# Graph layer in one pass over sorted edges: eight slot segments, clears in half-megabyte pieces, last layers in stages

## The chip, the cores and the metric

The kernel runs on one core of one Trainium2 chip. The metric is the time of one launch in microseconds (us), the median of several runs. A profiled execution, with its own time, stands beside them.

## The reference

There are 12500 nodes with 128 features, and 412500 edges (`src`, `dst`, 20 attributes, a weight), sorted by `dst`. All arithmetic is float32.

```python
h = jnp.maximum(_layernorm(x, axis=-1), 0.0)
# the graph layer, with idx_i = src (summed into) and idx_j = dst (gathered from)
hw  = h @ W_in2f
Wij = ssp(f_ij @ W_f1 + b_f1) @ W_f2 + b_f2        # ssp(x) = softplus(x) - log 2
x_ij = hw[idx_j] * (Wij * rcut_ij[:, None])
agg = jax.ops.segment_sum(x_ij, idx_i, num_segments=N)
out = ssp(agg @ W_o1 + b_o1) @ W_o2 + b_o2
return x + out
```

The gather runs over sorted nodes, so that neighbouring edges read neighbouring rows. The sum runs over `src`, which is in no order.

## The kernel before

**Edges to slots.** The edges are worked in order of `dst`, in 806 chunks of 512 (a *step* each); four chunks make a group, and there are 202 groups. For a chunk the kernel computes the edge messages (128 edges by 128 features, four times) and writes each message, with the place of its node within its block in a 129th column, to a row of its own in a table in HBM. A block is 128 nodes; there are 98 blocks, and four of them are a *quad* (25 quads). The row is found by counting: `rank` keeps in PSUM (`free`) how many rows of each block are taken. The write is an indirect DMA from GpSimd, four a step (L745; a *put* below), 3224 in all.

**Segments.** The groups are cut into segments (`SEGS`), each with its own slot table. In a table every block has `T` tiles of 128 rows (one more in the blocks where the segment's own `dst` range lies). With 64, 56, 32, 24, 14 and 12 groups, T is 12, 11, 7, 5, 3 and 3, and the tables have 1208, 1118, 710, 506, 310 and 304 tiles.

**Clears.** Rows that may stay unwritten must read as zeros. `clear` lists DMAs that write a zero tile over the middle part of every block's rows; a piece is at most 128 half blocks by ZN x ZR = 32 rows of 516 bytes, some 2.1 MB. The dict `zeros` holds at which step each is issued on SyncE's queue (L961): the first segment's before step 108, the second's from step 128 to 246, all others from 128 to 470. The first put into a segment waits for its clears (the first segment's for step 128).

**Collecting.** When a segment is full, `Collect` adds its table up: `load` (L783) brings a unit of up to 6 tiles into SBUF, `compare` (L794, VectorE) makes a 0/1 matrix from the 129th column, and `add` (L807, TensorE) multiplies: each tile adds into the accumulator `acc` of its quad. `acc` has one buffer. At a quad's end `keep` (L824, VectorE) adds it to the sums `agg`. The units of all segments but the last are spread over the steps by a planner, which works out a rate in tiles a step for each: 5.39 for the first segment (steps 265 to 488), and from then on 8.16 and 8.24. The last segment is collected after the last step.

**A step.** `step(k)` issues, in this order, on each engine in its own queue: the loads for later chunks and units; `blocks` for chunk k+7; `hidden_end` (L631); `window` (L706); `message` for chunk k (L739 and L741, which multiplies into one of four `o` tiles of two chunks each, then the four puts); `value` (L726, L730) and `picked` (L714, L719) for chunk k+1; `compare` of the units; `rank` for chunk k+6; `hidden`; `add` of the unit before; `rank_end`. At a segment's last chunk `rank_end` also reduces the counts for a flag (L693 to L701), and at a segment's first groups `columns` (L578 to L606) prepares new columns. This order is written out by hand (`tc.manual_schedule()`). `aside` runs `make_h` (layer norm and the first product) for later nodes beside the first 200 steps.

**After the last step.** The last segment's units are loaded, compared and added, and each finished quad goes through `finish`: load x on ScalarE's queue (L387), the product with W_o1 (L389), softplus (L366 to L373), the product with W_o2 (L398), two adds on VectorE (L401, L402) and the store (L403). This part stands outside the manual schedule: a scheduler places its instructions.

If the flag shows that a count went over a bound, a second way of computing everything (`anyway`) is run behind `tc.If`; it shares `finish`.

Of the kernel before, what the change touches and what calls it, by code (L numbers as in the profile page):

```python
# [9 lines left out]
F32 = mybir.dt.float32  # L10
# [4 lines left out]
ALU = mybir.AluOpType  # L15
PSUM = bass.MemoryType.PSUM

P = 128
TG = 16
CH = 512  # L20
NCHUNK = TG * P // CH
QT = CH // P
SEGS = (64, 56, 32, 24, 14, 12)
RW = P + 1
VIEWS = 16
BG = 8
ZR = 8
ZN = 4
WR = 32
UT = 6  # L30
BIG = float(1 << 11)
# [4 lines left out]
def ceil_div(a, b):  # L36
    return -(-a // b)
# [3 lines left out]
def gnn_kernel(  # L41
# [20 lines left out]
    nc = tc.nc  # L62
    N, D = x.shape
    NG, _, RBF, _ = f_t.shape
# [62 lines left out]
    NQ = ceil_div(N, QN)  # L127
# [15 lines left out]
    state = ctx.enter_context(tc.tile_pool(name="state", bufs=1))  # L143
# [13 lines left out]
    for c0 in range(0, NC, P):  # L157
        n = min(P, NC - c0)
# [14 lines left out]
    for q in range(NQ):  # L173
        cs = slice(quad_of.index(q), quad_of.index(q) + quad_of.count(q))
# [19 lines left out]
    wo2 = load(w_o2, [P, P], "wo2")  # L194
# [3 lines left out]
    bo2 = load(b_o2[None, :].to_broadcast([P, P]), [P, P], "bo2")  # L198
# [5 lines left out]
    def spread(t, n):  # L204
        return t[:, None, :].to_broadcast([t.shape[0], n, P])
# [14 lines left out]
    flag = const.tile([1, 1], I32, name="flag")  # L220
# [35 lines left out]
    bad = const.tile([1, NFLAG], F32, name="bad")  # L256
    nc.vector.memset(bad, 0.0)
    sums = tc.dram_tile([SUMT * P, P], F32, name="sums")
    segs = [Segment(k) for k in range(len(SEGS))]

# [107 lines left out]

    def softplus_end(a, r):

        nc.scalar.activation(a, a, AF.Exp, scale=-1.0)
        nc.scalar.activation(a, a, AF.Ln, bias=half, scale=0.5)
        nc.vector.tensor_add(r, r, a)  # L373

    def finish(t0, n, sT, edge, quad, psum):

        n0 = t0 * P
        full = min(n, N // P - t0)
        rest = N - n0 - full * P if full < n else 0
        xo = quad.tile([P, QT, P], F32, name="xo")  # L380
        pieces = []
        if full:
            pieces.append((P, slice(0, full), slice(n0, n0 + full * P)))
        if rest:
            pieces.append((rest, slice(full, n), slice(n0 + full * P, N)))
        for p, cs, rows in pieces:
            nc.scalar.dma_start(xo[:p, cs, :], x[rows, :].rearrange("(c p) f -> p c f", p=p))  # L387
        z = psum.tile([P, 2, CH], F32, name="z_out", tag="z")[:, 0, :n * P]
        nc.tensor.matmul(z, wo1, sT, start=True, stop=True)  # L389
        a = edge.tile([P, QT, P], F32, name="a_out")  # L390
        r = edge.tile([P, QT, P], F32, name="r_out")
        a_n = a[:, :n, :].rearrange("p c f -> p (c f)")
        r_n = r[:, :n, :].rearrange("p c f -> p (c f)")
        softplus_parts(a_n, r_n, z, bo1)
        softplus_end(a_n, r_n)
        v = psum.tile([P, QT, P], F32, name="v_out", tag="v", bufs=3)
        for i in range(n):
            nc.tensor.matmul(v[:, i, :], r[:, i, :], wo2, start=True, stop=True)  # L398
        for p, cs, rows in pieces:
            xi = xo[:p, cs, :]  # L400
            nc.vector.tensor_add(xi, xi, spread(bo2[:p, :], xi.shape[1]))  # L401
            nc.vector.tensor_add(xi, xi, v[:p, cs, :])  # L402
            nc.sync.dma_start(out[rows, :].rearrange("(c p) f -> p c f", p=p), xi)  # L403


    def anyway(edge, quad, psum):
        none = edge.tile([P, SUMT // parts * P], F32, name="none", bufs=1)
        nc.vector.memset(none, 0.0)
        rows = sums[:, :].rearrange("(p a c) f -> a p (c f)", p=P, a=parts)
# [3 lines left out]
        with tc.For_i(0, NG, 1) as g:  # L413
            f = edge.tile([P, CH], F32, name="f")
# [23 lines left out]
            for t in range(TG):  # L438
                c, i = divmod(t, QT)
# [19 lines left out]
                v = psum.tile([P, P], F32, name="v", bufs=3)  # L459
# [4 lines left out]
                m = quad.tile([P, P], F32, name="m")  # L464
# [9 lines left out]
        for t0 in range(0, NTILE, QT):  # L474
            n = min(QT, NTILE - t0)
            o = quad.tile([P, QT, P], F32, name="s_out")
            nc.sync.dma_start(o[:, :n, :], sums[t0 * P:(t0 + n) * P, :].rearrange("(c p) f -> p c f", p=P))
            tps = psum.tile([P, QT, P], F32, name="t_out", tag="nodes")
            for i in range(n):
                nc.tensor.transpose(tps[:, i, :], o[:, i, :], ident)  # L480
            sT = quad.tile([P, QT, P], F32, name="sT")
            nc.scalar.activation(sT[:, :n, :], tps[:, :n, :], AF.Copy)
            finish(t0, n, sT[:, :n, :].rearrange("p c f -> p (c f)"), edge, quad, psum)


    with tc.tile_pool(name="edge", bufs=2) as edge, tc.tile_pool(
        name="quad", bufs=3
# [3 lines left out]
        kept = {}  # L491
# [8 lines left out]
        def clear(seg):  # L500

            todo = []

            def put(b, e, low):

                half = seg.tiles(b) * P // 2
                v = seg.views[VIEWS][seg.row(b):seg.row(e), :].rearrange(
                    "(r c) f -> r (c f)", c=half)
                for q in range(0, 2 * (e - b), P):
                    n = min(P, 2 * (e - b) - q)  # L510
                    for r in range(low, half - low, ZN * ZR):
                        w = min(ZN * ZR, half - low - r)
                        todo.append((
                            v[q:q + n, r * RW:(r + w) * RW].rearrange("r (k f) -> r k f", f=ZR * RW),
                            zero[:n, None, :].to_broadcast([n, w // ZR, ZR * RW])))

            full = (NBLK - 1) // BG * BG
            for b, e in ((0, seg.b0), (seg.b0, min(seg.b1, full)), (seg.b1, full)):
                if b < e:
                    put(b, e, seg.low)  # L520

            for b in range(full, NBLK):
                low = seg.low if b < NBLK - 1 else seg.low_last
# [375 lines left out]
        zeros = {}  # L899
        units = {}  # L900
        collects = [Collect(seg) for seg in segs]
        AHEAD = 3

        seg = segs[0]
        todo = clear(seg)
        for i, d in enumerate(todo):
            zeros.setdefault(i * (seg.cleared - 20) // len(todo), []).append((seg, d))
        todo = clear(segs[1])
        for i, d in enumerate(todo):
            zeros.setdefault(seg.cleared + i * (seg.c1 - 10 - seg.cleared) // len(todo),  # L910
                             []).append((segs[1], d))
        todo = [(seg, d) for seg in segs[2:] for d in clear(seg)]
        for i, d in enumerate(todo):
            zeros.setdefault(segs[0].cleared + i * (segs[2].c0 - 10 - segs[0].cleared)
                             // len(todo), []).append(d)

        at = [seg.c1 + 9 for seg in segs[:-1]]
        work = [sum(seg.tiles(b) for b in range(NBLK)) for seg in segs[:-1]]
# [2 lines left out]
        while len(rate) < len(at):  # L921
            n = len(at) - len(rate)
            j = max(range(n), key=lambda j: sum(work[j:n]) / (end - at[j]))
# [25 lines left out]
        with tc.manual_schedule():  # L949
# [17 lines left out]
                step(k, now)  # L967
                next(aside, None)
            summed[0].add(summed[1])
        last = collects[-1]  # L970
        for u in range(len(last.units)):
            last.load(u)
            last.compare(u)
            last.add(u)
            for done in last.kept:
                finish(*done, edge, quad, psum)
            last.kept = []
        worst = state.tile([1, 1], F32, name="worst")
        nc.vector.tensor_reduce(worst, bad, axis=mybir.AxisListType.X, op=ALU.max)
        nc.vector.tensor_copy(flag, worst)  # L980

    missed = nc.values_load(flag[0:1, 0:1], min_val=0, max_val=P)
    with tc.If(missed > 0):
        with tc.tile_pool(name="any_e", bufs=2) as edge, tc.tile_pool(
            name="any_q", bufs=2
# [51 lines left out]
```

## Time and profile before

| what | value |
|---|---|
| time, median of 3 runs | 4383.54 us (4381.74 to 4402.45) |
| profiled execution, time and span | 4396.31 us, 4394.5 us |
| TensorE, VectorE, ScalarE, GpSimd busy | 82%, 71%, 53%, 71% |
| granted TensorE clock, mean | 0.855 |
| DMA | 829 MB, mean 189 GB/s |
| first put, last put (start) | 85.1 us, 4220.6 us |
| put, mean duration | 964 ns, x3224 |
| clears issued (L961) | 164, from 78.9 to 2441.6 us |

The profiled execution is 13 us above the median. PE is TensorE's matmuls, PEld its weight loads, DVE VectorE, ACT ScalarE, POOL GpSimd, SPq SyncE's DMA queue. A row of a group gives line, engine, operation, tiles, count, then busy time and mean duration, then the idle time before it and who ended that; a row of the waits gives who waited for whom, in all, how often, and the longest; a row of a table by stage gives a stretch, its length, each engine's busy time with its number of instructions, then the granted clock, the DMA engines' busy share and GB/s. Start times of single instructions are from the timeline.

### The profile page before, as it was taken

How to read it: one execution, taken by the hardware profiler on the slowest of the kernel's cores; microseconds unless marked ns; L12 is line 12 of the kernel's file. 1: busy time of each engine (PE TensorE's matmuls, PEld its weight loads, DVE VectorE, ACT ScalarE, POOL GpSimd, SP SyncE). 2: the span in 40 equal slices, each digit the busy share in tenths (PEclk: the TensorE clock that was granted, in tenths of full speed). 3: DMA queues.
4: the chain of work that ended last, by engine and by line, in shares of the span. 5: the costliest groups of instructions: out<-in, count | busy, mean ns of one | idle time of the engine just before them, and what ended most of it. 6: DMA issues, size and time to landing. Idle time of an engine off the chain costs nothing.

```text
span 4394.5 us, 72656 instructions
## 1 busy us (share of the span) xinstructions
PE 3607.4 (82%) x22558; PEld 2618.3 (60%) x22558; DVE 3140.1 (71%) x6637; ACT 2332.5 (53%) x4685; POOL 3114.6 (71%) x3288
## 2 busy tenths in 40 slices
PE   3767776777777888888788889999899998989877
PEld 2544444444444666666566567777677776767666
DVE  5766666566555776767667678787888878888766
ACT  3655555555555555555555555555555555545424
POOL 2777777677777777777777777777777777777620
PEclk9776666667666898899998899999999999999999
DMA  5766547888765666765876566666666766766666
GB/s 139 192 178 230 174 128 197 223 223 230 183 208 135 177 178 183 238 193 166 257 197 174 150 179 187 194 195 185 189 188 183 199 191 185 193 188 191 172 180 192
DMA packets 498071, 829.10 MB, mean 189 GB/s; under 512 B 170680, under 2 KB 288300, under 8 KB 497676
## 3 DMA queue, kind: packets, MB, share of 16 engines
q1 hardware_dynamic: 378950, 602.34, 51.2%
q0 software_dynamic: 103168, 213.15, 14.7%
q10 hardware_dynamic: 15558, 8.89, 0.7%
q8 instruction: 182, 2.98, 0.3%
q14 instruction: 213, 1.74, 0.1%
HBM read 425.03 MB, written 398.98 MB: 188 GB/s over the span
## 4 chain that ended last, share of the span: by engine, by line


## 5 line engine op out<-in xcount | busy, mean ns | idle before, releaser
L745 POOL DMA_INDIRECT slots<-o,slot x3224 | 3108.4, 964 | 1106.3 <-issue 803.6
L719 ACT ACTIVATE hg<-picked,rcut 128x128 f32<-128x128 f32 x3224 | 920.8, 369 | 1372.0 <-PE picked L714 1323.5
L807 PEld LDWEIGHTS acc<-to,m 128*128 128x128 f32 x8312 | 1078.7, 205 | 353.8 <-issue 187.7
L807 PE MATMUL acc<-to,m 128*128 128x128 f32 x8312 | 1154.6, 294 | 92.3 <-DVE agg L824 47.3
L730 PEld LDWEIGHTS v<-wf,r 128*128 128x128 f32 x6448 | 918.1, 220 | 303.7 <-issue 303.7
L730 PE MATMUL v<-wf,r 128*128 128x128 f32 x6448 | 1088.2, 320 | 0.0
L616 PE MATMUL z<-f,wf 20*128 20x512 f32 x1612 | 524.2, 726 | 217.5 <-DVE r L631 190.9
L794 DVE TENSOR_TENSOR to<-count_ps,m 128x768 f32<-128x768 f32 (+3 forms) x829 | 657.9, 812 | 51.8 <-PE acc L807 27.7
L619 ACT ACTIVATE a<-z,bf 128x1024 f32<-128x1024 f32 x403 | 449.1, 1114 | 426.7 <-PE z L616 426.7
L660 DVE TENSOR_REDUCE top<-free 128x4 f32<-128x392 f32 x806 | 447.2, 555 | 211.7 <-PE free L655 210.4
L631 DVE SCALAR_TENSOR_TENSOR r<-z,nbf,a 128x1024 f32<-128x1024 f32 x403 | 514.6, 1277 | 94.2 <-ACT a L625 92.5
L741 DVE TENSOR_TENSOR o<-v,hg 128x512 f32<-128x512 f32 x806 | 547.2, 679 | 2.8 <-ACT hg L719 2.1
L739 DVE COPY o<-place 128x8 f32<-128x8 f32 x403 | 80.4, 200 | 650.9 <-DMA slots<-o,slot 650.6
L714 PE MATMUL picked<-near,at 96*128 96x128 bf16 x3224 | 356.4, 240 | 218.0 <-DVE o L741 215.7
L625 ACT ACTIVATE a<-a,half 128x1024 f32<-128x1024 f32 x403 | 468.4, 1162 | 0.0
L636 DVE TENSOR_TENSOR inb<-count_ps,blk 128x392 f16<-128x392 f32 x806 | 445.7, 553 | 0.0
L726 PE MATMUL v<-bf_p,ones_b 3*128 3x512 bf16 x806 | 350.1, 434 | 104.1 <-DVE o L741 93.9
L620 ACT ACTIVATE a<-a 128x1024 f32<-128x1024 f32 x403 | 425.9, 1057 | 12.8
L714 PEld LDWEIGHTS <-at 96*128 96x128 bf16 x3224 | 275.7, 109 | 256.2 <-DVE o L741 224.6
L616 PEld LDWEIGHTS z<-f,wf 20*128 20x128 f32 x1612 | 142.4, 206 | 388.9 <-issue 186.3
L687 PE MATMUL free<-inb,rest_of 128*128 128x392 f16 x806 | 303.1, 376 | 55.0 <-DVE top L660 53.8
L706 DVE TENSOR_TENSOR at<-rel,prow 96x512 bf16<-96x512 bf16 x806 | 331.1, 411 | 0.0
(107 smaller groups left out, 1416.2 us busy)
## 6 DMA issues: line engine op xcount, KB each, us to landing
m<-slots SPq DMA_DIRECT2D x371, 387.0 KB
rel<-rel_d SPq DMA_DIRECT2D x202, 384.0 KB
m<-slots SPq DMA_DIRECT2D x172, 322.5 KB
m<-slots SPq DMA_DIRECT2D x212, 258.0 KB
slots<-o,slot POOLq DMA_INDIRECT x3224
slots<-zero SPq DMA_DIRECT2D x24, 2064.0 KB
f<-in_f_t SPq DMA_DIRECT2D x404, 80.0 KB
slots<-zero SPq DMA_DIRECT2D x22, 1032.0 KB
```

What stands on the lines that cost most here:

```text
L616: nc.tensor.matmul(z[:, k, :], wf1[rows, :], self.f[rows, :], start=True, stop=True)
L619: nc.scalar.activation(a, z, AF.Abs, bias=bf1)
L625: nc.scalar.activation(a, a, AF.Ln, bias=half, scale=0.5)
L631: nc.vector.scalar_tensor_tensor(r, z, nbf1, a, op0=ALU.max, op1=ALU.add)
L660: nc.vector.tensor_reduce(self.top[:, c * QT:(c + 1) * QT], free_v, axis=mybir.AxisListType.X, op=ALU.max)
L714: nc.tensor.matmul(ps[:, i, :], at[:, i * P:(i + 1) * P], near, start=True, stop=True)
L719: nc.scalar.activation(hg[:, i, :], ps[:, i, :], AF.Copy, scale=self.rcut[:, j:j + 1])
L730: nc.tensor.matmul(v[:, i, :], r[:, i * P:(i + 1) * P], wf2, start=False, stop=True, skip_group_check=True)
L741: nc.vector.tensor_mul(o[:, :, :P], v, hg)
L745: put = nc.gpsimd.indirect_dma_start(out=views[j % VIEWS], out_offset=bass.IndirectOffsetOnAxis(ap=self.slot[:, j:j + 1], axis=0), in_=o[: ...
L794: nc.vector.tensor_tensor(to[:, :n, :], count_ps[:, None, :].to_broadcast([P, n, P]), self.m[u][:, :n, P:].to_broadcast([P, n, P]), op=ALU ...
L807: nc.tensor.matmul(self.acc[b // QT][:, i, :], m[:, j, :P], to[:, j, :], start=t == 0, stop=t == self.seg.tiles(b) - 1)
```

## The change

Three things are changed.

- `SEGS` has eight segments instead of six. T becomes 13, 10, 6, 3, 3, 2, 2 and 2, and the tables have 1314, 1012, 612, 310, 310, 212, 204 and 206 tiles. The planner's rates become 6.32 tiles a step for the first segment (from step 281) and 8.235 from step 489 to the end. The segments with T = 3 are collected in steps 686 to 760, those with T = 2 in steps 761 to 811.
- `ZN` goes from 4 to 1, so that a clear is at most 0.53 MB. There are 636 of them with 158.5 MB, instead of 164 with 147.3 MB. A new loop spreads them evenly by number, in runs, so that each segment's are out before it needs them.
- `finish` becomes a generator with five `yield`s. After the last step, now inside the manual schedule, the stages of several quads are interleaved: while a quad's sums are added, the quad in front has its W_o1 product and activations, the one before that its softplus add, the one before that its W_o2 product, and the one before that the last add and the store. The x loads go to SyncE's queue two quads ahead, and b_o2 is added to x on GpSimd one quad ahead. The last segment's `compare` is one unit and its `load` three units ahead. The flag is reduced before this part.

```diff
-SEGS = (64, 56, 32, 24, 14, 12)
+SEGS = (68, 52, 30, 14, 14, 8, 8, 8)
-ZN = 4
+ZN = 1
...
-    def finish(t0, n, sT, edge, quad, psum):
+    def finish(t0, n, sT, quad, psum):
...
-        xo = quad.tile([P, QT, P], F32, name="xo")
+        xo = quad.tile([P, QT, P], F32, name="xo", bufs=6)
...
-            nc.scalar.dma_start(xo[:p, cs, :], x[rows, :].rearrange("(c p) f -> p c f", p=p))
+            nc.sync.dma_start(xo[:p, cs, :], x[rows, :].rearrange("(c p) f -> p c f", p=p))
+        yield
+        for p, cs, rows in pieces:
+            xi = xo[:p, cs, :]
+            nc.gpsimd.tensor_add(xi, xi, spread(bo2[:p, :], xi.shape[1]))
+        yield
...
         softplus_parts(a_n, r_n, z, bo1)
-        softplus_end(a_n, r_n)
+        softplus_logs(a_n)
+        yield
+        nc.vector.tensor_add(r_n, r_n, a_n)
+        yield
         v = psum.tile([P, QT, P], F32, name="v_out", tag="v", bufs=3)
         for i in range(n):
-            nc.tensor.matmul(v[:, i, :], r[:, i, :], wo2, start=True, stop=True)
+            nc.tensor.matmul(v[:, i, :], r_n[:, i * P:(i + 1) * P], wo2, start=True, stop=True)
+        yield
         for p, cs, rows in pieces:
             xi = xo[:p, cs, :]
-            nc.vector.tensor_add(xi, xi, spread(bo2[:p, :], xi.shape[1]))
             nc.vector.tensor_add(xi, xi, v[:p, cs, :])
             nc.sync.dma_start(out[rows, :].rearrange("(c p) f -> p c f", p=p), xi)
...
+        clears = [(seg, d) for seg in segs for d in clear(seg)]
+        due = [seg.cleared - 20 if seg is segs[0] else seg.c0 - 10 for seg in segs]
+        todo = [sum(seg is s for s, _ in clears) for seg in segs]
+        t0, i = 0, 0
+        while i < len(segs):
+            j = max(range(i, len(segs)), key=lambda j: sum(todo[i:j + 1]) / (due[j] - t0))
+            n = sum(todo[i:j + 1])
+            for m in range(n):
+                zeros.setdefault(t0 + m * (due[j] - t0) // n, []).append(clears.pop(0))
+            t0, i = due[j], j + 1
...
-        for u in range(len(last.units)):
-            last.load(u)
-            last.compare(u)
-            last.add(u)
-            for done in last.kept:
-                finish(*done, edge, quad, psum)
-            last.kept = []
...
+            for u in range(len(last.units)):
+                last.load(u + AHEAD)
+                if u + 1 < len(last.units):
+                    last.compare(u + 1)
+                if last.kept:
+                    last.kept = []
+                    go(q - 4)
+                last.add(u)
+                if last.kept:
+                    go(q + 2)
+                    go(q + 1)
+                    go(q - 1)
+                    go(q - 2)
+                    go(q - 3)
+                    q += 1
```

More of the change, by code (lines that the diff above doesn't have):

```diff
@@ L369, in softplus_end, with softplus_logs @@
     def softplus_end(a, r):
+        softplus_logs(a)
+        nc.vector.tensor_add(r, r, a)
+    def softplus_logs(a):
         nc.scalar.activation(a, a, AF.Exp, scale=-1.0)
         nc.scalar.activation(a, a, AF.Ln, bias=half, scale=0.5)
-        nc.vector.tensor_add(r, r, a)
-    def finish(t0, n, sT, edge, quad, psum):
+    def finish(t0, n, sT, quad, psum):
         n0 = t0 * P
@@ L386, in finish @@
         for p, cs, rows in pieces:
-            nc.scalar.dma_start(xo[:p, cs, :], x[rows, :].rearrange("(c p) f -> p c f", p=p))
+            nc.sync.dma_start(xo[:p, cs, :], x[rows, :].rearrange("(c p) f -> p c f", p=p))
[4 more added lines that the diff above has]
+        yield
         z = psum.tile([P, 2, CH], F32, name="z_out", tag="z")[:, 0, :n * P]
         nc.tensor.matmul(z, wo1, sT, start=True, stop=True)
[L390 to L393, printed above, removed]
+        a_n = quad.tile([P, 2, CH], F32, name="a_out", tag="a", bufs=2)[:, 0, :n * P]
+        r_n = quad.tile([P, 2, CH], F32, name="r_out", tag="r", bufs=3)[:, 0, :n * P]
         softplus_parts(a_n, r_n, z, bo1)
-        softplus_end(a_n, r_n)
+        softplus_logs(a_n)
+        yield
+        nc.vector.tensor_add(r_n, r_n, a_n)
+        yield
         v = psum.tile([P, QT, P], F32, name="v_out", tag="v", bufs=3)
         for i in range(n):
-            nc.tensor.matmul(v[:, i, :], r[:, i, :], wo2, start=True, stop=True)
+            nc.tensor.matmul(v[:, i, :], r_n[:, i * P:(i + 1) * P], wo2, start=True, stop=True)
+        yield
         for p, cs, rows in pieces:
             xi = xo[:p, cs, :]
-            nc.vector.tensor_add(xi, xi, spread(bo2[:p, :], xi.shape[1]))
             nc.vector.tensor_add(xi, xi, v[:p, cs, :])
@@ L482, in anyway @@
             nc.scalar.activation(sT[:, :n, :], tps[:, :n, :], AF.Copy)
-            finish(t0, n, sT[:, :n, :].rearrange("p c f -> p (c f)"), edge, quad, psum)
+            for _ in finish(t0, n, sT[:, :n, :].rearrange("p c f -> p (c f)"), quad, psum):
+                pass
     with tc.tile_pool(name="edge", bufs=2) as edge, tc.tile_pool(
@@ L902, in gnn_kernel @@
         AHEAD = 3
[L904 to L915, printed above, removed]
+        clears = [(seg, d) for seg in segs for d in clear(seg)]
[8 more added lines that the diff above has]
+            t0, i = due[j], j + 1
         at = [seg.c1 + 9 for seg in segs[:-1]]
@@ L969, in gnn_kernel, with go @@
             summed[0].add(summed[1])
-        last = collects[-1]
-        for u in range(len(last.units)):
-            last.load(u)
-            last.compare(u)
-            last.add(u)
-            for done in last.kept:
-                finish(*done, edge, quad, psum)
-            last.kept = []
-        worst = state.tile([1, 1], F32, name="worst")
-        nc.vector.tensor_reduce(worst, bad, axis=mybir.AxisListType.X, op=ALU.max)
-        nc.vector.tensor_copy(flag, worst)
+            worst = state.tile([1, 1], F32, name="worst")
+            nc.vector.tensor_reduce(worst, bad, axis=mybir.AxisListType.X, op=ALU.max)
+            nc.vector.tensor_copy(flag, worst)
+            last = collects[-1]
+            outs = []
+            for b in range(0, NBLK, QT):
+                n = min(QT, NBLK - b)
+                sT = kept["agg"][:, b:b + n, :].rearrange("p c f -> p (c f)")
+                outs.append(finish(b, n, sT, quad, psum))
+            def go(q):
+                if 0 <= q < NQ:
+                    next(outs[q], None)
+            go(0)
+            go(1)
+            for u in range(AHEAD):
+                last.load(u)
+            go(0)
+            last.compare(0)
+            q = 0
+            for u in range(len(last.units)):
[13 more added lines that the diff above has]
+                    q += 1
+            for q in range(NQ, NQ + 5):
+                go(q - 4)
+                go(q - 1)
+                go(q - 2)
+                go(q - 3)
     missed = nc.values_load(flag[0:1, 0:1], min_val=0, max_val=P)
```

## The prediction

> **What bounds the kernel now.** I read the page first (span, busy shares, the costliest group), then GpSimd's waits, GpSimd's timeline, a table by stage, the waits of one late stage, and TensorE's timeline of the tail.
>
> ```profile
> span 4394.5 us, 72656 instructions
> L745 POOL DMA_INDIRECT slots<-o,slot x3224 | 3108.4, 964 | 1106.3 <-issue 803.6 <-DVE o L741 109.4 <-DMA slots<-o,slot 96.7
> ```
>
> The 3224 scatters ("puts", four a step, 806 steps) hold GpSimd 3108.4 us, and with the idle time before them 4215 us: nearly the whole span.
>
> ```profile
> POOL slots L745 <- issue: 803.6, 2632, 0.9
> POOL slots L745 <- DVE o L741: 109.4, 48, 78.2
> POOL slots L745 <- DMA slots<-o,slot: 96.7, 245, 4.4
> ```
>
> Most of that idle time waits for nothing: 0.305 us between two puts. The median distance of two put starts is 1.263 us. The first starts at 85.1, the last at 4220.6 and ends at 4221.6; 3223 x 1.263 = 4070.7 of the 4135.5 between. So there is 65 us of stall before the last put, and a tail of 172.9 us after it. Nothing in the change makes a put cheaper: only these two can change. By stage (four puts a step), steps 182 to 754 run at 1.2692 us a put, 5.08 a step. Steps 104 to 182 take 422.9 us for 312 puts: 26.9 too many. Steps 754 to the last put take 277.9 for 207: 15.2 too many.
>
> ```profile
> core 0: us, PE busy (x) PEld busy (x) DVE busy (x) ACT busy (x) POOL busy (x), PEclk, DMA share, GB/s
> 615.90:1038.80 422.90, 307.84 (x1406) 189.76 (x1406) 254.29 (x640) 225.09 (x461) 301.05 (x313) 0.65 0.76 206
> 1038.80:3942.70 2903.90, 2503.82 (x16414) 1860.15 (x16413) 2147.68 (x4360) 1574.02 (x3156) 2205.08 (x2288) 0.89 0.67 189
> 4040.90:4176.60 135.70, 118.16 (x806) 92.01 (x806) 105.66 (x205) 67.06 (x136) 95.89 (x100) 0.92 0.63 173
> 4235.00:4384.00 149.00, 119.49 (x843) 101.85 (x842) 103.30 (x148) 58.96 (x95) 0.00 (x0) 0.98 0.72 208
> ```
>
> The slow early stage (first row) has TensorE at 73% and VectorE at 60%; what stands out is the DMA share.
>
> **Clears.** What stalls there is this kind of gap:
>
> ```profile
> 794.75 0.96 POOL L745 DMA_INDIRECT slots<-o,slot  x1 [0.31 <-issue]
> 800.09 0.95 POOL L745 DMA_INDIRECT slots<-o,slot  x1 [4.38 <-DMA slots<-o,slot]
> ```
>
> In the compiled order each put waits for the landing of the put eight before it, issued 10.1 us earlier. A clear of up to 2.1 MB that is queued in one piece takes the 16 engines 2.1 MB / 0.27 MB per us = 8 us (206 GB/s at 0.76 busy is 271 full), and two were issued together at 784.3. The DMA load by itself does not stall: steps 390 to 416 moved 240 GB/s at 0.79 busy with 1.2716 us a put, but at 0.24 MB of clears a step, against 0.44 to 0.56 MB in the stalled steps 104 to 208. By the new planner all 636 pieces come out in a single run of 0.83 pieces a step to step 766: 0.22 MB a step in 104 to 182, none over 0.53 MB. I take the whole 26.9 away: -27 (bounds 0, if it isn't the size, and -30 with the 2.8 us of the first 104 steps). It adds 11.3 MB and 472 issues; a clear's issue is 0.45 us in the median, about 0.4 us a step on SyncE's queue in front of the m and near loads, which lead their use by steps: 0, or up to +8 where a late stage has no reserve. The late steps, which had no clears, now get about 0.2 MB / 5.08 us = 39 GB/s on 189, the load of steps 390 to 416: 0.
>
> The Trainium skill ("DMA: Bandwidth & Descriptors", Bandwidth and Anatomy of one DMA) speaks against this edit: about 2 us fixed per DMA, and a rule to batch to 1 MiB or more. Paid one after the other, 472 more DMAs would be an estimated +944 us by that page; no run here shows it yet, and the sum doesn't use it.
>
> **Segments.** Tiles per block T go from 12, 11, 7, 5, 3, 3 to 13, 10, 6, 3, 3, 2, 2, 2. The tiles collected inside the loop rise from 3852 to 3974, at the same top rate (8.24 tiles a step, now from step 489 on). What differs is the end of a quad: `keep` adds its 128x512 accumulator (L824, 0.67 us), and with a single "acc" buffer TensorE and VectorE meet there. At T=3 a quad ends 0.7 times a step (17 in the 24 steps below), at T=2 once.
>
> ```profile
> ACT hg L719 <- PE picked L714: 53.4, 25, 6.1
> DVE agg L824 <- PE acc L807: 29.1, 15, 4.7
> POOL slots L745 <- DVE o L741: 11.0, 5, 3.8
> ```
>
> These are the waits of 4040.9 to 4176.6, the only T=3 collection in the loop (steps 774 to 798): the add waits 29.1 us for TensorE. To price it I take the "lead", from the start of a step's L741 to its first put in the timeline. It is 28 us while VectorE is stopped by the four o buffers; when it is gone GpSimd waits. Pace of L741: T=6, 4.70 us a step (3958.8 to 4034.0, 16 steps); T=5, 5.17 (3733.1 to 3924.4, 37 steps); T=3, 5.65 (24 steps; 5.12 over the first nine, 5.96 over 784 to 798). The T=3 row's granted clock of 0.92 is worth 0.08 x 135.7 = 10.9 us, 0.45 a step: 5.20 without. At 0.96, the clock of the 98 us before, 0.2 comes back: 5.40. T=2 has 0.3 quad ends a step more; from T=6 (0.35 a step, 4.70) to T=3 (0.71, 5.20) a quad end costs 0.50 / 0.36 = 1.4 us: 5.82.
> Now the sum. T=3 covers steps 686 to 760: 75 x (5.40 - 5.08) = 24. T=2 covers 761 to 806: 46 x 0.74 = 34. A segment's last `rank_end` and the next `columns` take 3 to 5 us of lead (at 601, 697 and 753); four of them from 706 on: 16. Together 74, less 24 of the 26 us lead that T=6 should leave at 686: 50 us of stall where 15 stand now: +35 (bounds +1 and +103, below). Earlier stages had 25 us of lead or more: 0.
>
> **Tail.** The last segment falls from 304 tiles to 206, and `finish` is cut in stages, so that TensorE need not wait within one quad.
>
> ```profile
> 4302.62 2.84 PE L807 MATMUL acc<-to,m 128*128 128x128 f32 x24
> 4306.57 1.16 PE L398 MATMUL v_out<-wo,r_out 128*128 128x128 f32 x8 [1.10 <-DVE r_out L373]
> 4307.56 1.02 PE L389 MATMUL z_out<-agg,wo 128*128 128x512 f32 x2
> 4308.42 0.83 PE L807 MATMUL acc<-to,m 128*128 128x128 f32 x6
> ```
>
> A quad now takes 5.80 us (4302.62 to 4308.42): 2.84 of sums, 0.99 of v, 0.86 of z, and 1.1 waiting for r. With 8 tiles the sums take 1.89: 3.74 in all for TensorE. VectorE: 2 compares of 0.61, three adds of 0.6: 3.0. ScalarE 2.6. DMA: 8.24 tiles x 66 KB + 0.51 MB = 1.06 MB, 3.7 us at 286 GB/s (208 at 0.72, full), 5.1 at 208. I take 4.5, between the two and over TensorE. 13.4 us pass before the first compare of the last segment and 10.1 after the last sum (4384.4), as now: 13.4 + 25 x 4.5 + 10.1 = 136 against 172.9: -37 (4.1 us a quad: -47; 5.3: -17). The x loads move from ScalarE's queue to SyncE's: 0.4 us a quad on a queue that has 4 issues in 4.5 us; out stores wait there for the add of a quad four back, with three units loaded ahead: 0. The bo2 add moves to GpSimd, which no row prices; the add on VectorE is 0.66, GpSimd's largest plain row is 0.95 (L255). It has two quads of time and GpSimd nothing else: 0, or 25 x 0.3 = 8 if it had to be waited for. The flag's reduction (0.3 us) is 0.
>
> The Trainium skill ("GPSIMD Engine Reference", Performance versus the Vector engine) has a two-input add there 1.96 times slower than on VectorE: estimated 1.3 us, +16 us if it lay on the path. Here it is off it.
>
> **Sum.** -27 + 35 - 37 = -29. The profiled execution took 4396.3 us (span 4394.5), 13 over the median of the runs; against the median 4383.5 the forecast is 4355.
>
> **Rivals.** *Thin segments ride along*: T=3 keeps the 5.12 of its first nine steps, T=2 5.54: 3 + 21 + 16 - 24 - 15 = +1, in all -63: 4320. For it: TensorE was idle for 13% of the T=3 row; against it: 5.96 when the lead was gone. *The loop turns TensorE-bound (slower)*: T=3 at 5.96 and T=2 at 6.38 give 66 + 60 + 16 - 24 - 15 = +103: +39, 4422. It decides from a mean pace of about 5.98 over steps 686 to 806 on. For it: idle TensorE loses its clock (0.92 in the T=3 row, 0.96 before). *The clears' size isn't it*: the stall stays with make_h's traffic: -2, 4382.
>
> **Chances.** Forecast 0.42, riding along 0.20, TensorE-bound 0.20, clears 0.18. 0.5% (22 us) is about what a measurement of this kernel can tell from no change. Under 4361.6: 0.29 of the forecast, 0.20, 0.04 of the clears: 0.53. Over 4405.4: 0.17 of TensorE-bound and 0.03 of the rest: 0.20. Between: 0.27. Range 4310 (riding along with 4.1 us a quad) to 4412 (part of TensorE-bound); the forecast's own is 4335 to 4375, by the tail's bounds.
>
> **What would show it.** Right: 1.27 us a put in steps 104 to 182; the last put near 4231; after it 136 us, a quad every 4.5; GpSimd waiting for L741's successor only after about step 730. Wrong: waits on put landings remaining early (clears); a lead that never falls to 1 us (riding along); stalls from step 700 on and a clock under 0.92 (TensorE-bound); m loads that VectorE waits for in the tail (DMA price too low).

## The result and the profile after

| | before | after |
|---|---|---|
| median of 20 runs each | 4383.92 us (4376.67 to 4402.45) | 4400.18 us (4391.16 to 4410.39) |
| ratio to before | 1 | 1.0035, 95% interval 1.0027 to 1.0043 |
| profiled execution, time and span | 4396.31 and 4394.5 us | 4407.69 and 4406.0 us |
| last put ends | 4221.6 us | 4269.9 us |
| tail after it | 172.9 us | 136.1 us |

The changed kernel is 16 us slower; 4355 was forecast, 29 us faster. The lines of after that answer to those of before follow in the same order: first the page's span and GpSimd's group row of the put (now L757; lines from `finish` on stand 12 further down):

```profile
span 4406.0 us, 73576 instructions
L757 POOL DMA_INDIRECT slots<-o,slot x3224 | 3144.0, 975 | 1119.0 <-issue 788.2 <-DVE o L753 159.1 <-DMA slots<-o,slot 79.0
```

The idle time grew by only 13 us, but the busy time of the same 3224 puts by 35.6 us (3144.0 against 3108.4): each is longer. The median put is 0.968 us against 0.958. The 10th percentile went from 0.954 to 0.964 and the 90th from 0.961 to 0.971, so nearly every put is longer; the usual gap between two is still 0.305. Most of the 35.6 us is this shift (3224 x 0.010 = 32).

GpSimd's waits in the early stage (steps 104 to 182):

```profile
POOL slots L757 <- issue: 77.8, 255, 0.3
POOL slots L757 <- DMA slots<-o,slot: 11.6, 38, 0.3
```

No put waits for a landing any more beyond the usual gap of 0.3 us (before, 30 waits of up to 4.4 us, 29.8 in all).

The table by stage: steps 104 to 182; the T=3 stage (steps 686 to 760, by L753); most of the T=2 stage; the middle of the tail. The columns are those of the prediction's table.

```profile
core 0: us, PE busy (x) PEld busy (x) DVE busy (x) ACT busy (x) POOL busy (x), PEclk, DMA share, GB/s
617.30:1018.70 401.40, 310.07 (x1448) 191.78 (x1447) 259.43 (x650) 231.37 (x476) 306.27 (x313) 0.67 0.55 159
3576.60:4000.50 423.90, 366.91 (x2476) 285.17 (x2475) 329.09 (x641) 203.25 (x407) 300.52 (x309) 0.91 0.69 202
4011.50:4255.40 243.90, 203.42 (x1382) 156.08 (x1382) 192.40 (x392) 111.99 (x228) 161.26 (x167) 0.94 0.59 161
4285.00:4396.00 111.00, 93.28 (x629) 76.69 (x630) 74.61 (x116) 60.15 (x97) 28.48 (x23) 0.98 0.70 212
```

The early stage takes 21.5 us less, with the DMA engines 55% busy instead of 76%. In the T=3 stage L753 comes every 423.9 / 74 = 5.73 us, TensorE is busy for 87% of it at a clock of 0.91; in the T=2 stage every 243.9 / 42 = 5.81 us.

The waits of the T=2 stage (4010 to 4260):

```profile
DVE agg L836 <- PE acc L819: 46.9, 38, 4.9
POOL slots L757 <- DVE o L753: 37.0, 17, 4.8
PEld acc L819 <- DVE agg L836: 25.0, 23, 3.1
```

VectorE and TensorE wait for each other at the one accumulator, 38 and 23 times, and the puts wait for VectorE's L753 behind them.

TensorE in the tail:

```profile
4318.00 1.16 PE L819 MATMUL acc<-to,m 128*128 128x128 f32 x8 [0.59 <-DVE to L806]
4319.00 1.02 PE L399 MATMUL z_out<-agg,wo 128*128 128x512 f32 x2
4319.86 1.05 PE L409 MATMUL v_out<-wo,r_out 128*128 128x128 f32 x8
4320.75 1.06 PE L819 MATMUL acc<-to,m 128*128 128x128 f32 x8
4322.56 1.16 PE L819 MATMUL acc<-to,m 128*128 128x128 f32 x8 [0.76 <-DVE to L806]
```

A quad takes 4.56 us; the wait for r is gone, and what is left is a wait for the compare.

**Where the time went.** Taking only what GpSimd was idle beyond 0.305 us between two puts, by stage (us; where it is over 0.15):

| | steps 104-182 | 702-754 | 754 to the end | tail | first put | puts longer | span |
|---|---|---|---|---|---|---|---|
| before | 26.2 | 0.0 | 16.1 | 172.9 | 85.1 | | 4394.5 |
| after | 0.0 | 29.1 | 32.0 | 136.1 | 81.3 | 35.6 | 4406.0 |
| difference | -26 | +29 | +16 | -37 | -4 | +36 | +11.5 |

The differences add up to +14, where the span grew by 11.5. The first four columns sum to -18, with the first put to -22; the longer puts turn that into a loss.

### The profile page after: what moved, and what is told of

Same layout as the page of the kernel before. It is cut to its first block, busy times and chain, and to the rows that moved or that the text cites. A ratio compares the mean times of both kernels' runs of the same rounds, so it can differ in the third digit from the quotient of the medians.

```text
span 4406.0 us, 73576 instructions
## 1 busy us (share of the span) xinstructions
PE 3673.4 (83%) x22606; PEld 2659.3 (60%) x22606; DVE 3169.9 (72%) x6744; ACT 2333.4 (53%) x4685; POOL 3182.4 (72%) x3314
## 4 chain that ended last, share of the span: by engine, by line
## 5 line engine op out<-in xcount | busy, mean ns | idle before, releaser
L757 POOL DMA_INDIRECT slots<-o,slot x3224 | 3144.0, 975 | 1119.0 <-issue 788.2
L819 PE MATMUL acc<-to,m 128*128 128x128 f32 x8360 | 1184.0, 295 | 186.1 <-DVE to L806 109.4
L742 PEld LDWEIGHTS v<-wf,r 128*128 128x128 f32 x6448 | 941.5, 225 | 323.5 <-issue 323.5
L742 PE MATMUL v<-wf,r 128*128 128x128 f32 x6448 | 1114.7, 325 | 0.0
L628 PE MATMUL z<-f,wf 20*128 20x512 f32 x1612 | 536.5, 743 | 202.1 <-DVE r L643 183.3
L806 DVE TENSOR_TENSOR to<-count_ps,m 128x640 f32<-128x640 f32 (+3 forms) x873 | 662.3, 783 | 53.4 <-DMA m<-slots 39.7
L753 DVE TENSOR_TENSOR o<-v,hg 128x512 f32<-128x512 f32 x806 | 548.2, 680 | 0.3 <-issue 0.2
```

The costliest lines, as they stand in the source:

```text
L628: nc.tensor.matmul(z[:, k, :], wf1[rows, :], self.f[rows, :], start=True, stop=True)
L742: nc.tensor.matmul(v[:, i, :], r[:, i * P:(i + 1) * P], wf2, start=False, stop=True, skip_group_check=True)
L753: nc.vector.tensor_mul(o[:, :, :P], v, hg)
L757: put = nc.gpsimd.indirect_dma_start(out=views[j % VIEWS], out_offset=bass.IndirectOffsetOnAxis(ap=self.slot[:, j:j + 1], axis=0), in_=o[: ...
L806: nc.vector.tensor_tensor(to[:, :n, :], count_ps[:, None, :].to_broadcast([P, n, P]), self.m[u][:, :n, P:].to_broadcast([P, n, P]), op=ALU ...
L819: nc.tensor.matmul(self.acc[b // QT][:, i, :], m[:, j, :P], to[:, j, :], start=t == 0, stop=t == self.seg.tiles(b) - 1)
```

## The experiments

The theory: the clears and the tail gain what was forecast, the thin segments cost somewhat more, and the rest of the loss is that the puts are longer because the b_o2 add is on GpSimd. Rivals: the longer puts come from the clears, the segments or the traffic they bring; or the segments alone explain the loss.

Runs e5 to e8 (one chip), f1 to f4 (another) and g1 (a third) were on chips where the kernel before itself takes 5863 to 5894 us in the median. In its profile there (e6) GpSimd waits 1625 us for VectorE's `o`, and the granted TensorE clock is 0.746 instead of 0.855; why these chips differ is not shown. So of these runs only the length of the puts and the tail are read. Ratios are to the kernel before on the same chip. A median put is that of the 3224 records in the one profile of a run; on those chips it is 0.962 or 0.971 (once 0.967, e7) where the other runs show 0.958 to 0.960, or 0.967 to 0.968.

### One part at a time

**e1: the changed kernel with the add on VectorE**

```diff
-            nc.gpsimd.tensor_add(xi, xi, spread(bo2[:p, :], xi.shape[1]))
+            nc.vector.tensor_add(xi, xi, spread(bo2[:p, :], xi.shape[1]))
```

> The changed kernel with the bo2 add of finish back on VectorE; all else as changed. Theory (the add on GpSimd makes every put longer): the median put falls back from 0.968 to 0.958 us, the distance of two puts from 1.273 to 1.263, and the time by about 3224 x 0.010 = 32 us, to about 4368; the tail stays within 3 us. Rival (tables, clears or the execution lengthen the put): put stays at 0.968, time within 5 us of 4400.

Measured: 4384.61 us (ratio to before 0.9978, 0.9962 to 0.9995), puts 0.958, tail 138.9. The puts have the length of before, while segments, clears and staging are those of after: these alone do not lengthen them. The kernel is 12 us faster than before on this chip, where the whole change had been forecast to bring 29.

**e2: the kernel before with the add on GpSimd**

```diff
-            nc.vector.tensor_add(xi, xi, spread(bo2[:p, :], xi.shape[1]))
+            nc.gpsimd.tensor_add(xi, xi, spread(bo2[:p, :], xi.shape[1]))
```

> The kernel before, with only the bo2 add of finish moved to GpSimd. Theory (the add on GpSimd makes every put longer): put median 0.968 instead of 0.958, distance 1.273, time about +30 us (4414), although the adds come after the last put. Rival (something else lengthens the put): 0.958, time within 5 us of before, or up to 15 us less, since VectorE loses 17 us of adds in the tail.

Measured: 4390.46 us (0.9985, 0.9968 to 1.0002), tail 164.0. GpSimd's group row:

```profile
L745 POOL DMA_INDIRECT slots<-o,slot x3224 | 3115.6, 966 | 1074.7 <-issue 809.1
```

The median put is 0.960, as in e3 and e4 on the same chip, which have no such add: the add on GpSimd does not lengthen the puts in every program, and the theory's 0.968 did not come. In `before` the last layers stand outside the hand-written order, and the scheduler moved three of the 26 adds ahead of the first put (at 85.3 us):

```profile
18.58 2.49 POOL L401 TENSOR_TENSOR xo<-xo,bo 128x512 f32<-128x512 f32 x2 [11.74 <-DMA xo<-in_x]
21.35 1.26 POOL L401 TENSOR_TENSOR xo<-xo,bo 128x512 f32<-128x512 f32 x1 [0.28 <-DMA xo<-in_x]
```

So here GpSimd ran the same add both before and after its puts, and they stayed short.

**e3: the clears alone** (`ZN = 1` and the new loop for `zeros`, in the kernel before)

```diff
-ZN = 4
+ZN = 1
...
```

> The kernel before, with only the clears changed: pieces of at most 0.53 MB, spread evenly by the new planner. Theory (queued big clears delay the landing of puts): steps 104 to 182 fall from 422.9 us to about 397, time about -25 us (4359), put median 0.958. Rival (the pieces, or their number, lengthen every put): put median 0.968, the 32 us that this costs eat the gain, time 4384 to 4395.

Measured: 4383.31 us (0.9972, 0.9954 to 0.999), 13.5 us under before, where about 25 were expected; puts 0.960. Steps 104 to 182 took 399.6 us against 422.9, without stall; there are 2 us of stall in steps 494 to 702 and 4 in 702 to 754 that before does not have, and the puts hold GpSimd 13 us longer (3121.3 us).

**e4: the segments alone**

```diff
-SEGS = (64, 56, 32, 24, 14, 12)
+SEGS = (68, 52, 30, 14, 14, 8, 8, 8)
```

> The kernel before, with only SEGS changed to eight segments. Theory (thin tables end a quad more often and turn the late loop TensorE-bound): steps 702 to the last put lose about 45 us more than before, the tail gets 98 tiles x 0.236 = 23 us shorter, time +15 to +25 us, put median 0.958. Rival for the longer put (the tables): put median 0.968 and another +32 us. Rival for the late loop (clears in late steps stall it): with the old clears, all out by step 470 or so, the late loop loses under 25 us.

Measured: 4430.63 us (1.0074, 1.0047 to 1.0102), 34 us over before. Stall from step 702 on is 60.1 us against 16.1; the tail is 147.6 (206 tiles instead of 304, unstaged); puts 0.960. The steps before 494 stall 39 us instead of 29, with the large clears of before and more bytes to clear. Alone, this is the one part of the three that makes the kernel slower.

**e5, e6: the changed kernel and the kernel before again**, without an edit.

> The changed kernel once more, on the chip that the other kernels of this call run on. Theory (the put's 0.968 us belongs to this program): put median 0.968 again, distance 1.273, time about 30 us above the same kernel with the add on VectorE. Rival (it belonged to the chip or the execution): put median 0.958 to 0.960 as in the four other programs, time at or a little below before.

> The kernel before once more, for the length of its put on the chip of this call. Theory (the program sets it): 0.958 again. Rival (the chip sets it): the same value as the changed kernel's in this call, within 0.001.

Measured: 5930.21 us and 5844.86 us, puts 0.971 and 0.962, tails 140.4 and 173.9. The difference in the puts is there on this chip too, while GpSimd waits 1716 and 1625 us for VectorE's `o`.

**e7: the staged last layers alone** (segments and clears as before, `finish` and the code that runs its stages as after)

```diff
-SEGS = (68, 52, 30, 14, 14, 8, 8, 8)
-ZN = 1
+SEGS = (64, 56, 32, 24, 14, 12)
+ZN = 4
...
```

> The kernel before with the staged last layers alone; segments and clears as before. Theory (in the tail TensorE waits 1.1 us a quad for r): a quad falls from 5.80 to about 4.7 us, the tail from 172.9 to about 146, time -27. Rival (DMA bounds the tail): 12.2 tiles a quad are 1.32 MB, at 208 GB/s 6.3 us a quad: tail within 5 us of 172.9. For the put: 0.958 to 0.960 if the add on GpSimd is not it, 0.968 if adds staged behind the puts are.

Measured: 5853.26 us (0.9989, 0.9967 to 1.0012), puts 0.967 against the 0.962 of e6 and the 0.971 of e5, tail 168.8 against 173.9. The tail of 146 that the theory gave did not come; the rival, a tail within 5 us, did. Steps of 0.002 to 0.005 between programs, such as these two or 0.958 against 0.960 elsewhere, are not explained.

**e8 and e9: the changed kernel with the six segments of before**, on two chips

```diff
-SEGS = (68, 52, 30, 14, 14, 8, 8, 8)
+SEGS = (64, 56, 32, 24, 14, 12)
```

> The changed kernel with the six segments of before: clears in small pieces and staged layers stay. Theory (the thin segments cost more in the loop than they bring in the tail): steps 702 to the last put come back to about 545 us from 592, the tail is about 146 instead of 136, so 25 to 35 us less than the changed kernel and 45 to 50 less than before. Rival (thin segments pay): time above the changed kernel's.

> The changed kernel with the six segments of before, on another chip than the last call's. Theory (the thin segments cost more in the loop than they bring in the tail): steps 702 to the last put take about 545 us instead of 592, the tail about 146 instead of 136: time 25 to 35 us under the changed kernel; with the longer put (0.968) about 20 us under before, without it about 50. Rival (thin segments pay): above the changed kernel.

Measured: e8 5853.71 us (0.9989, 0.9967 to 1.001), puts 0.971, tail 172.2. e9 4383.96 us (0.9985, 0.9972 to 0.9999), puts 0.967, stall from step 702 on 21.6 us, tail 162.5. The tail of about 146 came on neither chip: staging without fewer tiles brings 10 us in e9, and 5 and 2 in e7 and e8 (against e6). The middle of e9's tail in the table by stage, and what VectorE waits for in it:

```profile
4248.00:4386.00 138.00, 117.11 (x836) 99.87 (x836) 88.58 (x123) 60.17 (x97) 31.84 (x24) 0.99 0.72 216
```
```profile
DVE to L806 <- DMA m<-slots: 41.8, 36, 4.2
```

The waits for r are gone, but the units now arrive late: 216 GB/s against 208 before and 212 after. The tail moves its bytes at nearly the same rate in all three, which fits a tail that is shorter mainly where there are fewer tiles to load. That the DMA engines set this rate is not shown by a run of its own.

**e10: the same with the add on VectorE** (both edits, e1's and e9's)

> The same with the bo2 add on VectorE. Theory (the add on GpSimd, behind the puts, lengthens them here): put median 0.010 us under that of the kernel with the add on GpSimd, time 30 us under it, about 45 to 50 us under before; the tail up to 3 us longer. Rival (the put's length belongs to the chip): the same put, time within 5 us of the one with the add on GpSimd.

Measured: 4371.62 us (0.995, 0.9932 to 0.9967), puts 0.958, tail 169.1. This version is faster than both kernels: 19.5 us under before on the same chip. Moving the add to VectorE costs 6.6 us in the tail and brings 0.009 us on every put; staging then brings only 4 us against before's 172.9.

**e11, e12: the changed kernel again, and once more with the add on VectorE** (e1's edit), on the chip of e9 and e10

> The changed kernel again. Theory (the longer put belongs to this program): put median 0.968, as before on two chips; time 10 to 20 us over before. Rival (it belongs to chips): within 0.001 of the kernel with the add on VectorE in this call, time under before.

> The changed kernel with the add on VectorE again, for its put on the chip of this call. Theory (the program sets it): 0.958, 0.010 under the changed kernel. Rival (the chip sets it): the same as the changed kernel's here.

Measured: e11 4403.42 us (1.0023, 1.001 to 1.0037), puts 0.967; e12 4384.55 us (one run; e1, the same kernel, has 4384.61 in 12 runs), puts 0.958. GpSimd's group row of e11, then of e12:

```profile
L757 POOL DMA_INDIRECT slots<-o,slot x3224 | 3140.7, 974 | 1128.4 <-issue 799.6
```
```profile
L757 POOL DMA_INDIRECT slots<-o,slot x3224 | 3110.5, 965 | 1126.8 <-issue 800.5
```

The idle time is the same within 2 us; the busy time differs by 30.2, and the launch time by 19: the tail is 4 us shorter in e11 (134.5 against 138.7), and the profiled executions differ by 28. From e12 to e10, where only the segments differ, the time falls by another 13 us; from e11 to e9, by 19.

### What makes the puts longer

**f1, f2: the add on GpSimd only in `anyway`, which is not entered, or only in the last layers that run** (`finish` gets the engine as `adder`; f1's diff, f2 has the two engines exchanged)

```diff
-            for _ in finish(t0, n, sT[:, :n, :].rearrange("p c f -> p (c f)"), quad, psum):
+            for _ in finish(t0, n, sT[:, :n, :].rearrange("p c f -> p (c f)"), quad, psum, nc.gpsimd):
...
-                outs.append(finish(b, n, sT, quad, psum))
+                outs.append(finish(b, n, sT, quad, psum, nc.vector))
```

> The changed kernel, with the bo2 add of the last layers on VectorE in the part that runs, and on GpSimd only in the second way of computing, which is not entered. If the mere presence of GpSimd's add among its instructions makes each put longer: put median 0.967 us, span some 4405 us. If the add has to be run, or to be wired into the staged part (its waits and semaphores): 0.958 us and a span of some 4380 us, as with all adds on VectorE.

> The changed kernel, with the bo2 add on GpSimd in the staged last layers that run, and on VectorE in the second way of computing, which is not entered. If the 26 adds that run are what counts: put median 0.967 us, span some 4405 us. If the adds of the second way count: 0.958 us. If it is a matter of the number of GpSimd's instructions: between the two.

Measured: puts 0.962 in f1, 0.971 in f2 (5957.14 and 5948.38 us, one run each; the expected spans do not apply on this chip). The adds of the last layers count, those of the second way do not.

**f3: the add of one quad alone on GpSimd**

```diff
...
+                outs.append(finish(b, n, sT, quad, psum, nc.gpsimd if b == 0 else nc.vector))
```

> The changed kernel, with the bo2 add of the first quad alone on GpSimd, all others on VectorE. If one such add is enough (an operation that GpSimd has to have at hand): put median 0.967 us. If the effect goes with their number: 0.958 us.

Measured: 5952.06 us (one run), puts 0.971. The group rows of f1 and of f3:

```profile
L757 POOL DMA_INDIRECT slots<-o,slot x3224 | 3110.7, 965 | 2693.9 <-DVE o L753 1782.2
```
```profile
L757 POOL DMA_INDIRECT slots<-o,slot x3224 | 3142.9, 975 | 2651.3 <-DVE o L753 1734.7
```

One add, run after the last put, has the whole effect: 32.2 us of busy time. The effect does not go with the number of adds.

**f4: 26 memsets on GpSimd after the last put instead**

```diff
...
+            for _ in range(26):
+                nc.gpsimd.memset(zero, 0.0)
```

> The changed kernel with all bo2 adds on VectorE, and 26 memsets of a 128x1032 tile on GpSimd after the last put, whose result is not needed. If any 26 more instructions behind the puts lengthen them (where the program lies in memory): put median 0.967 us. If it is the two-input add, or its tie to the x loads: 0.958 us. The memsets run beside the tail; the span should be that of the kernel with the adds on VectorE, some 4380 us plus 8 us if the puts are longer by a quarter of that.

Measured: 5949.87 us (one run), puts 0.962. Just any further instructions on GpSimd behind the puts are not the cause.

**g1: the changed kernel with the x loads on ScalarE's queue**

```diff
-            nc.sync.dma_start(xo[:p, cs, :], x[rows, :].rearrange("(c p) f -> p c f", p=p))
+            nc.scalar.dma_start(xo[:p, cs, :], x[rows, :].rearrange("(c p) f -> p c f", p=p))
```

> The changed kernel, with the bo2 add on GpSimd, and the x loads of the last layers on ScalarE's queue, as they were before. In the kernel before, the add on GpSimd left the puts at 0.960 us; there the x loads were on ScalarE's queue and the last layers were not staged. If it is the tie to a load on SyncE's queue: put 0.958 to 0.962 us, the time 25 to 30 us under that of the changed kernel. If it is the add among the staged, hand-ordered instructions: put 0.967 to 0.971 us, and the time of the changed kernel, give or take 5 us.

Measured: 5927.33 us (1.0114, 1.005 to 1.0177), puts 0.971, tail 135.1. There is no profile of a kernel with short puts from this chip; 0.971 is the value of the long puts on the two other chips of this kind, and the time is over before's as in e5 (1.0136). So the queue of the x loads is not what makes the difference from e2.

**h1: all adds of the last layers on VectorE, one add on GpSimd before the loop**

```diff
...
         with tc.manual_schedule():
+            nc.gpsimd.tensor_add(zero[:, :CH], zero[:, :CH], zero[:, :CH])
```

> The changed kernel with all bo2 adds of the last layers on VectorE, and one 128x512 add of the zero tile to itself on GpSimd, in place, at the head of the hand-written order, before the first put; its result is still zero. If an add on GpSimd anywhere in the hand-written order lengthens the puts: 0.967 to 0.971 us. If it must stand behind the puts, among the staged last layers: 0.958 to 0.962 us, as with all adds on VectorE.

Measured: 4407.96 us (1.0041, 1.0008 to 1.0073), puts 0.967. The add in the zero tile's instructions (shortest, median and longest duration in ns, start in us), and the group row of the puts:

```profile
L962 POOL TENSOR_TENSOR zero<-zero x1: 1039/1039/1039, 6.9 to 6.9; 128x512 f32<-128x512 f32 x1
```
```profile
L757 POOL DMA_INDIRECT slots<-o,slot x3224 | 3141.3, 974 | 1118.2 <-issue 800.5
```

One add of 1.04 us, some 75 us before the first put, costs what all 26 cost: the puts have 3141.3 us, e12's (on another chip) 3110.5. Nothing runs beside the puts that did not before, so it is no contention with the add. But for e7, which lies between, the kernels fall in two groups. Long puts: those with a two-input add on GpSimd within the hand-written order, wherever it stands. Short puts: those without one, or with one only outside that order (e2, where it runs, and f1, where it does not). That the hand-written order is what counts rests on e2 alone, which is the kernel before; no run has such an add run outside that order in the changed kernel. What carries the effect stays open. The order and the waits of GpSimd's instructions up to the last put are the same in e1 and in the changed kernel. That an add has been run is not enough (e2), and in f3 the only add of a launch starts after its last put.

## Why the prediction was wrong

**The step that failed** is "Nothing in the change makes a put cheaper: only these two can change", and with it the price of the add, "0, or 25 x 0.3 = 8 if it had to be waited for". The text looked for what the add itself takes and whether something waits for it, and there it was right: its row in the tail is

```profile
L395 POOL TENSOR_TENSOR xo<-xo,bo 128x512 f32<-128x512 f32 x24 | 31.4, 1309 | 82.6 <-DMA xo<-in_x 71.3 <-DVE r_out L405 5.9 <-DVE agg L836 5.4
```

with a median of 1.27 us, 1.9 times VectorE's 0.66. The Trainium skill ("GPSIMD Engine Reference", Performance versus the Vector engine) has a ratio of 1.96, from which 1.3 us was estimated, and agrees. But the cost was not there. It was about 0.010 us on each of 3224 puts: 30 us of GpSimd's time in e11 against e12, and in h1 as much with none of the 26 adds on GpSimd. Of the launch time it is 19 us (e11 against e12) to 25 (after against e1, each by its ratio to before). No row of before could give this price; what could have been seen is that the sum took the most frequent instruction's duration as fixed, where a hundredth of a microsecond is worth as much as the whole forecast.

**Clears: the amount right, the reason not isolated.** -27 was forecast, and the stall of steps 104 to 182 went from 26.2 to 0.0; alone, e3 shows -23 in that stage. The puts do land earlier: from a put's start to the last update of its semaphore, the 90th percentile in steps 130 to 156 fell from 11.3 us, over the 10.1 us that eight puts take, to 4.6. But the change makes the pieces smaller and also thins them out in this stage, from 0.52 to 0.21 MB of clears a step; no run does one alone. The row with which the text set the load apart was misread. Steps 390 to 416 of before (2095.6 to 2227.9 us) issued not 0.24 but 0.47 MB of clears a step:

```profile
slots<-zero SPq DMA_DIRECT2D x5, 2064.0 KB
slots<-zero SPq DMA_DIRECT2D x2, 774.0 KB
```

These largest pieces, one at a time and 14 to 22 us apart, stalled no put. In the stalled steps they came mostly in pairs of up to 2.6 MB, beside other loads. So a piece of 2.1 MB alone is not enough; how much of the stall belongs to the size, to the pairs and to the load is not shown.

Here the Trainium skill ("DMA: Bandwidth & Descriptors", Bandwidth and Anatomy of one DMA) speaks for batching to 1 MiB or more, for the sake of bandwidth; e3, with pieces of at most 0.53 MB and 404 more DMAs, is 13.5 us faster. The stall of e3 from step 494 on, 7 us more than before's, lies within the "0, or up to +8" of the text.

**Segments: right in kind, too low, and in part by luck.** +35 was forecast, and the stall from step 702 on rose by 61.1 - 16.1 = 45. T=3 came at 5.73 instead of 5.40: (5.73 - 5.40) x 74 = 24 us too little. The term at fault is the correction for the clock: the row of before was taken to run at 0.96, and measured was 0.91 in this stage; the uncorrected row (5.65) was nearer. The lead at step 686 was 19 us, not 24 to 26, and was gone at step 711, not after 730. On the other side, the 16 us for segment ends are already in these paces: 74 x 0.65 + 46 x 0.73 - 19 = 63, where 61 were measured. That T=2 came at 5.81 us a step, where 5.82 was forecast, is luck: the forecast stood on the 5.40 and added 0.42 for more quad ends, and from T=3 to T=2 the measured pace rose by only 0.08, at a clock of 0.94 after 0.91. The price of 1.4 us for a quad end is not confirmed.

**Tail: the sum right, its parts not seen.** 136 was forecast and 136.1 measured, at 4.56 us a quad where the text said 4.5. But fewer tiles bring 25 us of it without staging (e4), and staging without fewer tiles brings 2 to 10 (e7 to e10). The 4.5 was picked between two prices for the loads, and the hit does not confirm it: VectorE does wait for units in the staged tail (29.5 us in the tail of after), the sign that the text gave for a DMA price too low. It did not show in the sum.

**The rivals.** *Thin segments ride along* falls: the lead was used up and the stall rose. *The clears' size isn't it* falls as a forecast, since the 26 us of stall went; whether it was the size is not shown. *The loop turns TensorE-bound* gave the right sign, but not by its price: the mean pace from 3576.6 to 4255.4 was 5.75 us a step, under its 5.98, and the segments cost 45, not 103. Its sign, a clock under 0.92 and stalls from step 700 on, is met in the T=3 stage (0.91). It does not by itself explain the loss: with the same segments and the add on VectorE, e1 is 12 us faster than before.

By the measured terms: clears -26, late stall +45, tail -37, first put -4, puts +36, together +14, where the spans differ by 11.5 and the medians by 16. Without the longer puts the sum is -22, short of the -29 mainly by the segments.

## What to carry to other kernels

Before pricing what an edit adds, look at what its kernel does thousands of times. After such a change, compare the duration of that instruction first: 1% of it was worth some 30 us here, more than the 26 us of stall that the clears cost. An instruction put on an otherwise unchanged engine can cost something where it does not run; undoing just that move is a cheap test, and here e10, without the add on GpSimd and without the thin segments, kept the gain (0.995, 0.9932 to 0.9967). Where two edits meet in one stage, forecast each alone: of the tail's 37 us fewer tiles were 25.

## What the runs showed of the hardware

- One two-input 128x512 add on GpSimd within the hand-written order makes the indirect DMA issues of this kernel longer in the median, from 0.958 to 0.967 us (0.962 to 0.971 on other chips), whether it stands before them or after them. 26 memsets there do not, nor did 26 adds outside that order in the kernel before (0.960, as in e3 and e4 without them).
- The kernel before took 4384 to 4397 us in the median on some chips and 5863 to 5894 us on others. In the profile of a slow one an indirect DMA issue took 0.962 us against 0.958, GpSimd waited for VectorE's output for 1625 us instead of 109, and the granted TensorE clock was 0.746 instead of 0.855.
- With clears of at most 0.53 MB, 0.21 MB a step, the last semaphore update of a put came within 4.6 us nine times in ten (steps 130 to 156); with pieces of 0.40 to 1.85 MB, many in pairs and 0.67 MB a step in all, within 11.3. Single pieces of 2.1 MB, 0.47 MB a step with the smaller ones, gave 7.8 in steps 390 to 416 and no stall.
